# A graph layer and a mixture of experts on one core: stages of a tile closer together, and another list of expert steps

## The chip, the core and the metric

The kernel runs on one core of a Trainium2 chip. The metric is the device time of one execution in microseconds. The core has five engines that run side by side, each in the order of its own instructions: PE (matrix multiply), DVE (vector), ACT (activation), POOL (here it issues the gathers, the read-backs and some stores) and SP (it issues the other transfers).[...]

## What is computed

6250 nodes with 256 features pass a graph layer over 106,250 edges (sorted by target), and then a layer of 8 experts of which each node uses 2:

```python
x = x + gnn(layernorm(x), deg_isqrt, W, b, src, dst)    # h @ W.T + b, gathered by src, summed by dst
x = x + ffn(layernorm(x), Wg, bg, W1, b1, W2, b2)

def ffn(x):
    topk_scores, topk_idx = top_k(x @ Wg.T + bg, 2)
    combine = softmax(topk_scores) spread over the 8 experts
    for e in range(8):
        h = relu(x @ W1[e].T + b1[e])                   # 256 -> 1024
        out = out + combine[:, e] * (h @ W2[e].T + b2[e])
```

All inputs are float32. In the graph layer the sum over edges is taken first and the 256x256 matrix is applied to the sums.

## The kernel before

**Head.** `in_order` counts the degrees, scales the rows and writes them as a table of two float16 halves to DRAM (`ftable`).

**Gathering.** The edges lie in 831 chunks of 128. The loop over the chunk number `s` does for each chunk: `gather` six chunks ahead (POOL, line 404, 128 rows of 1 KB into one of `ROWS` = 24 buffers), `mask` ten chunks ahead (DVE, line 411), and `add_up` (PE, line 418), a matmul of mask and rows that sums the edges of each node in PSUM. Then it issues what was planned for this chunk number, and then pieces of expert work.

**Stages of a tile.** A tile is 128 nodes; there are 49. Tile t is complete at chunk `FROM[t]`, about every 17 chunks. From there its stages are planned at fixed distances in chunks, by `plan_at` and the list `STAGES`:

- `join` (DVE) adds finished windows of the sum, `part_of` (ACT) copies them into a whole tile.
- `turn_sum` (PE) transposes the tile, `keep_turned` (ACT) copies it, `linear` (PE, line 518) applies the matrix and the gate.
- `add_sums`, `guess_root`, `better_root`, `score_nodes`, `choose_experts`, `scale_rows` (all DVE, lines 525 to 582): residual, layer norm, scores, the two experts of each node.
- `rank` (PE, lines 586 and 587): counts per expert, and on ACT a float16 copy of the normalised rows.
- `place_rows`, `place_sorted`, `place_queued`, `mark_slots`, `weigh` (DVE): places in the experts' queues, and a one-hot matrix of sorted slots.
- `sort` (PE, line 650) brings the rows into expert order, `send_rows` copies them (ACT) and writes 64 rows to each expert's queue in DRAM (SP, eight transfers, `fhq`).

`linear` stands 8 chunks before `rank`, `rank` 6 before `sort`, and the rows are sent 24 chunks after `FROM[t]`. The PSUM tile `pt` of `turn_sum`, `linear` and `rank` has one buffer.

**Expert steps.** A step takes up to 128 or 256 rows of one queue. `STREAM` lists the steps of the gathering as (chunk number at which the step is chosen, rows); `TAIL` lists the rows of those chosen after the last tile is sent. `choose` (DVE) takes the expert with most waiting rows. SP then loads the weights (`w1` of 1028 KB by `load_first`, `w2` of 1152 KB by `load_second`, three buffers each) and the rows (`xT` by `load_rows`, after a register load of the column). A step that finds fewer rows than it may take costs the same. The work is cut into pieces: 8 `up` pieces for a step (line 766, with a relu on ACT) and 4 `down` pieces for each 128 rows (line 776); `leave` adds the bias (DVE, line 788) and writes the result to DRAM (`fyq`, SP). `next_kind` alternates the two kinds where both are at hand; where only `down` is, it holds it back when the next `up` is due within `HOLD` = 10 chunks. `earliest` keeps the first `up` of a step at least 13 chunks after its choice and 12 chunks after the last sending that it needs. A credit of `SLOT` = 1250 ns a chunk limits how many pieces are issued.

**Tail.** After chunk 831 the loop goes on with one piece in each round of `s`; planned stages fall due by the same count. `DONE` pairs a step with a tile number: once the step is done, all tiles below the number are taken to be complete. Then `read_back` (POOL, line 859) fetches two expert results for each node, `add_in` (DVE, line 867) adds them, and `store` writes four tiles. `take`, which calls `add_in`, runs in a round where the oldest read-back is eight rounds old, where more than ten are open, or where the `down` pieces of all steps have been issued (`done == USUAL`). Before the last read-backs the kernel checks that no row was written later than `DONE` says; if one was, `any_order`, a slower general program, recomputes everything.

Of the kernel before, what the change touches and what calls it, by code (L numbers as in the profile page):

```python
# [12 lines left out]
SP = mybir.EngineType.SP  # L13
ACT = mybir.EngineType.Activation
AF = mybir.ActivationFunctionType
# [4 lines left out]
P = 128  # L20
N = 6250
NT = 49
# [11 lines left out]
FT = 256  # L34
CAP = 27 * FT
QR = NE * CAP
SLOTS = 64
STREAM = ((74, 128), (83, 128), (94, 128), (103, 128), (112, 128), (121, 128), (130, 128), (139, 128),
          (148, 128), (175, 256), (194, 256), (213, 256), (232, 256), (249, 256), (266, 256), (283, 256),
          (300, 256), (317, 256), (333, 256), (350, 256), (367, 256), (384, 256), (401, 256), (418, 256),  # L40
          (435, 256), (452, 256), (469, 256), (486, 256), (503, 256), (520, 256), (537, 256), (554, 256),
          (572, 256), (589, 256), (606, 256), (623, 256), (640, 256), (657, 256), (674, 256), (691, 256),
          (705, 256), (721, 256), (738, 256), (756, 256), (773, 256), (790, 256), (807, 256), (825, 256),
          (839, 256))
TAIL = (256, 256, 256, 256, 256, 128, 128, 128, 128, 128, 128)
ROWS_OF = [n for s, n in STREAM] + list(TAIL)
USUAL = len(ROWS_OF)
START = [P + sum(ROWS_OF[:step]) for step in range(USUAL + 1)]
# [20 lines left out]
SHARED = 4  # L69
SHIFT = 1.0 / 16  # L70

DONE = ((40, 25), (41, 27), (43, 28), (44, 31), (45, 32), (47, 33), (48, 35), (50, 37), (52, 38), (53, 40),
        (54, 42), (56, 44), (57, 45), (58, 46), (USUAL - 1, NT))
LATER = 1 << 17
TURNED, PLACED, SORTED, SENT = 5, 17, 22, 24
LEAD = (13, 12)
HOLD = 10


COPIES = 3  # L80
# [70 lines left out]
def in_order(ctx: ExitStack, tc: tile.TileContext, g: Shared):  # L151

    nc = tc.nc
# [4 lines left out]
    hq = dram.tile([NE * P, CAP, 2], F32, name="fhq")  # L158
# [209 lines left out]
    t0 = 0  # L368
    for step, t1 in DONE:
        nc.vector.memset(bounds[:, t0:t1, :], float(START[step + 1]))  # L370
# [213 lines left out]
    def rank(r):  # L584
        r.pp = psp.tile([P, 3, NE], F32, name="pt", bufs=1)
        nc.tensor.matmul(r.pp[:, 0], below, r.chose[:, 0], start=True, stop=True)
        nc.tensor.matmul(r.pp[:, 1:3], every, r.chose, start=True, stop=True)
        h2s[r.t] = work.tile([P, 2, D], F16, name="h2s", bufs=3)
        nc.scalar.activation(h2s[r.t][:, 0], r.h2, AF.Copy)

    def place_rows(r):

# [14 lines left out]
    def place_sorted(r):  # L607
        scr = work.tile([P, NE], F32, name="scr")
        r.slotf = work.tile([P, 2], F32, name="slotf")
        for j in range(2):  # L610
            nc.vector.scalar_tensor_tensor(scr, r.sel[:, j], 1.0, r.spot, op0=OP.mult, op1=OP.mult,
                                           accum_out=r.slotf[:, j:j + 1])
        nc.vector.tensor_copy(columns_of[r.t][:, 1], r.totals[0:1, 1])
        if r.t == NT - 1:
            nc.vector.tensor_scalar(r.slotf, r.slotf, dump, None, op0=OP.add)
        nc.scalar.activation(r.ex, r.ex, AF.Exp)

    def place_queued(r):

# [33 lines left out]
    def send_rows(r):  # L653
# [3 lines left out]
        send(r.t)  # L657
        sent += 1

    STAGES = ((9, add_sums), (10, guess_root), (11, better_root, 2), (12, better_root, 1), (12, score_nodes),  # L660
              (13, choose_experts), (14, scale_rows), (16, rank), (PLACED, place_rows), (18, place_sorted),
              (19, place_queued), (20, mark_slots), (21, weigh), (SORTED, sort), (SENT, send_rows))

    def send(t):

# [54 lines left out]
    def load_first(step):  # L720
        f = steps[step]
        f["we"] = nc.values_load(f["go"][0:1, 0:1], engines=(SP,), min_val=0, max_val=(NE - 1) * P)
        f["w1"] = wts.tile([P, W1C], F32, name="w1")
        nc.sync.dma_start(f["w1"], g.W1[bass.ds(f["we"], P), :])

    def load_rows(step):

        f = steps[step]
        assert sent >= f["known"]
        col = nc.values_load(f["go"][0:1, 1:2], engines=(SP,), min_val=0, max_val=CAP - FT)  # L730
        f["xT"] = work.tile([P, FT, 2], F32, name="xT", bufs=4)
        n = ROWS_OF[step]
        nc.sync.dma_start(f["xT"][:, :n, :], hq[bass.ds(f["we"], P), bass.ds(col, n), :])  # L733

    def load_second(step):
        f = steps[step]
        f["w2"] = wts.tile([P, W2C], F32, name="w2")
        nc.sync.dma_start(f["w2"], g.W2[bass.ds(f["we"], P), :])
# [60 lines left out]
    def plan_at(s, fn, *args):  # L799
        tasks.setdefault(s, []).append((fn, args))  # L800

    def run(parts):
        for _ in parts:
            pass

    def in_parts(s, fn, *args):

        def part(s):
            if next(parts, True) is None:
                tasks.setdefault(s + 1, []).insert(0, (part, (s + 1,)))  # L810
        parts = fn(*args)
        plan_at(s, part, s)

    earliest, busy = {}, {}
    taken_up = set()
    for t, s in enumerate(FROM):
        plan_at(s + TURNED, turn_sum, t)
        plan_at(s + TURNED + 1, keep_turned, t)
        plan_at(s + TURNED + 3, linear, t)
        r = Shared()  # L820
        r.t = t
        for at_slot, stage, *args in STAGES:
            plan_at(s + at_slot, stage, r, *args)
        taken_up.update(range(s + SORTED, s + SENT + 1))
        for at_slot, task in ((s + TURNED, "turn_sum"), (s + TURNED + 3, "linear"), (s + PLACED - 1, "rank"),
                              (s + SORTED, "sort")):
            busy[at_slot] = busy.get(at_slot, 0) + TASKS[task]
    for w, (n0, chunks) in enumerate(WINDOWS):
        tasks.setdefault(chunks[-1] + 2, []).insert(0, (join, (w,)))
        plan_at(chunks[-1] + 4, part_of, w)  # L830
    plan_at(3, centre)
    s = 1
    for t in range(0, NT, 2):
# [5 lines left out]
        for at_slot, task in ((s, "inputs_turned"), (s + 2, "inputs_scored")):  # L839
            busy[at_slot] = busy.get(at_slot, 0) + TASKS[task]  # L840
    for step, (s, n) in enumerate(STREAM):
        in_parts(s, fetch, step)
        last = max(t for t in range(NT) if FROM[t] + PLACED < s)
        earliest[step] = max(s + LEAD[0], FROM[last] + SENT + LEAD[1])
    chosen = loaded1 = loaded2 = len(STREAM)
    all_sent = FROM[NT - 1] + SENT + 1

    curu = curd = 0
    done = gone = upped = 0
# [28 lines left out]
    def next_kind(s):  # L878

        first = upped < USUAL and upped <= done + 1 and "xT" in steps.get(upped, {}) and s >= earliest.get(upped, 0)  # L880
        second = done < upped and "w2" in steps.get(done, {})
        if first and second:
            return "down" if was == "up" else "up"
        if first:
            return "up"
        soon = 0 < earliest.get(upped, 0) - s <= HOLD and upped <= done + 1 and curd == 0
        return "down" if second and not soon else None

    def next_piece(s):

# [14 lines left out]
    with tc.manual_schedule():  # L905
# [21 lines left out]
        with tc.tile_pool(name="ftail", bufs=2) as pool:  # L927
            s = NC
            pend = []
            plan = list(DONE)  # L930
            got = asked = allowed = stored = 0
# [12 lines left out]
            while done < USUAL or tasks or len(plan) > 1 or asked < 2 * allowed or pend:  # L944
                for fn, args in tasks.pop(s, []):
                    fn(*args)
                if s > all_sent and s > max(STREAM)[0] + 6:
                    if chosen < min(USUAL, upped + 4):
                        run(choose(chosen))
                        chosen += 1  # L950
                    if loaded2 < min(loaded1, gone + 3):
                        load_second(loaded2)
                        loaded2 += 1
                    if loaded1 < min(chosen, upped + 3):
                        load_first(loaded1)
                        load_rows(loaded1)
                        loaded1 += 1
                over = done
                next_piece(s)
                if done > over:  # L960
                    since[over] = s
                if len(plan) > 1 and done > plan[0][0] and s >= since.get(plan[0][0], 0) + 6 \
                        and asked == 2 * allowed:
                    step, t1 = plan.pop(0)
                    results(allowed, t1, float(START[step + 1]))
                    allowed = t1
                    latest = step
                if asked < 2 * allowed and s % (4 if s > all_sent else 2):
                    pend.append((s, read_back(pool, rowat, asked // 2, asked % 2, latest)))
                    asked += 1  # L970

                if pend and (done == USUAL or len(pend) > 10 or s >= pend[0][0] + 8):
                    take()
                s += 1

# [559 lines left out]
```

## Time and profile before

| | |
|---|---|
| median of 3 timed runs | 1579.9 us (1570.63 to 1580.15) |
| profiled execution, own time | 1342.39 us |
| its span in the trace | 1340.5 us |
| mean granted PE clock in it | 0.959 |
| busy share PE, DVE, ACT, POOL | 86%, 74%, 30%, 67% |
| first and last gather start | 81.7 us, 1126.1 us |
| last segment sum starts on PE | 1136.67 us |

The durations below are those of the profiled execution, which is shorter than the timed runs. "Busy" is the time that an engine spends in instructions; a group of the page is given by line, engine, operation, output and inputs, then its count, its busy time and mean, and the idle time before it with what ended it. Line numbers of the trace are those of the kernel before.

### The profile page before, as it was taken

The page shows a single profiled execution, that of the slowest core. Times are in us where ns is not written, and L with a number is a line of the kernel's source. Part 1 is how long each engine was busy: PE and PEld are TensorE (multiplying, and loading weights), DVE is VectorE, ACT ScalarE, POOL GpSimd, SP SyncE. Part 2 cuts the span into 40 slices and gives each one's busy share as a digit, 9 for nine tenths or more (in the row PEclk, how much of TensorE's full clock was granted, in tenths as well). Part 3 has the DMA queues.
Part 4 walks back from the last instruction along what each step waited for, and adds up shares of the span by engine and source line. Part 5 has one row for each costly group of instructions (what it writes and reads, how often), then busy time and mean ns, then how long its engine had stood idle before and what let it go on. Part 6 is the DMA issues. An engine that isn't in the chain of part 4 may idle for free. (4 is left out here: it accounts for less than half of the span.)

```text
span 1340.5 us, 24208 instructions
## 1 busy us (share of the span) xinstructions
PE 1154.7 (86%) x6304; PEld 896.9 (67%) x6304; DVE 986.4 (74%) x5416; ACT 397.6 (30%) x939; POOL 903.2 (67%) x983
## 2 busy tenths in 40 slices
PE   4439978997879999999989898999999998979992
PEld 4427656774657777676767666767777666868881
DVE  9841668787788888878888887978777775875532
ACT  2622323332323333233323232333222222312230
POOL 2047777777777777777777777777777775557423
PEclk9999867998989999999999999999999998989996
DMA  8343468997778888888888888888888887699783
GB/s 297 112 145 105 121 192 300 337 338 229 226 232 279 262 256 271 252 272 259 256 258 251 268 251 265 257 257 265 255 273 273 252 260 248 218 343 337 272 323 98
DMA packets 159197, 333.81 MB, mean 249 GB/s; under 512 B 26804, under 2 KB 105864, under 8 KB 143688
## 3 DMA queue, kind: packets, MB, share of 16 engines
q1 hardware_dynamic: 111372, 201.66, 44.0%
q0 software_dynamic: 46864, 129.82, 32.8%
q8 instruction: 52, 0.85, 0.3%
q14 instruction: 97, 0.79, 0.2%
q10 hardware_dynamic: 812, 0.68, 0.2%
HBM read 277.55 MB, written 54.50 MB: 248 GB/s over the span
## 5 line engine op out<-in xcount | busy, mean ns | idle before, releaser
L404 POOL DMA_INDIRECT rows<-ftable,src x831 | 790.8, 952 | 253.4 <-issue 115.5
L766 PE MATMUL ph<-xT,w 128*128 128x256 f32 (+1 forms) x1920 | 468.4, 368 | 36.4 <-DMA xT<-fhq 36.1
L776 PE MATMUL py<-w,hid 128*128 128x256 f32 x1680 | 436.9, 383 | 2.3 <-DVE y L788 1.7
L766 PEld LDWEIGHTS ph<-xT,w 128*128 128x128 f32 x1920 | 342.8, 193 | 138.8 <-issue 54.4
L768 ACT ACTIVATE hid<-ph,w 128x256 f32<-128x256 f32 (+1 forms) x480 | 214.3, 447 | 712.9 <-PE ph L766 625.1
L418 PE MATMUL ps<-rows,mask 128*128 128x512 f16 x831 | 309.9, 400 | 79.4 <-DMA rows<-ftable,src 74.6
L776 PEld LDWEIGHTS py<-w,hid 128*128 128x128 f32 x1680 | 317.5, 191 | 86.5 <-issue 20.9
L411 DVE TENSOR_SCALAR mask<-col_b,rel 128x128 f16<-128x128 bf16 x831 | 208.3, 272 | 8.3 <-PE ps L418 8.2
L859 POOL DMA_INDIRECT yb<-fyq,rowat x98 | 94.7, 966 | 84.8 <-issue 33.0
L418 PEld LDWEIGHTS <-mask 128*128 128x128 f16 x831 | 84.6, 105 | 77.4 <-issue 39.9
L788 DVE TENSOR_TENSOR y<-py,w 128x256 f32<-128x256 f32 x105 | 44.3, 422 | 93.9 <-PE py L776 92.3
L867 DVE SCALAR_TENSOR_TENSOR xr<-yb,prob,xr 128x256 f32<-128x256 f32 x98 | 46.0, 482 | 63.2 <-DMA yb<-fyq,rowat 62.5
L485 DVE SCALAR_TENSOR_TENSOR rolled<-rolled,keep,ps 128x256 f32<-128x256 f32 x149 | 70.6, 474 | 14.9 <-PE ps L418 14.8
L500 ACT ACTIVATE whole<-rolled 32x256 f32<-32x256 f32 (+2 forms) x156 | 63.7, 408 | 17.3 <-DVE rolled L488 14.8
L525 DVE SCALAR_TENSOR_TENSOR xr<-pt,norm,xr 128x256 f32<-128x256 f32 x49 | 23.6, 481 | 61.5 <-PE pt L518 61.5
L488 DVE TENSOR_TENSOR rolled<-ps,rolled 128x256 f32<-128x256 f32 x150 | 63.6, 424 | 5.1
L518 PE MATMUL pt<-gw,uT 128*128 128x264 f32 x196 | 54.8, 405 | 0.0
L518 PEld LDWEIGHTS pt<-gw,uT 128*128 128x128 f32 x196 | 39.3, 201 | 16.9 <-issue 6.8
L217 PE MATMUL count<-oh,ol 128*16 128x8 bf16 (+2 forms) x898 | 29.0, 174 | 21.9 <-DVE oh L206 17.9
L461 PEld LDWEIGHTS ph<-wg,turned 128*128 128x128 f32 x196 | 37.2, 279 | 15.4 <-ACT turned L453 14.2
L469 POOL MEMSET keep<- 128x1 f32 x11 | 0.4, 96 | 64.3 <-DMA ftable<-tab 64.3
L217 PEld LDWEIGHTS <-ol 128*16 128x16 bf16 x898 | 28.7, 109 | 22.2 <-DVE ol L203 16.1
(187 smaller groups left out, 1154.7 us busy)
## 6 DMA issues: line engine op xcount, KB each, us to landing
w<-in_W SPq DMA_DIRECT2D x60, 1152.0 KB
w<-in_W SPq DMA_DIRECT2D x60, 1028.0 KB
fhq<-ordered SPq DMA_DIRECT2D x392, 64.0 KB
fyq<-y SPq DMA_DIRECT2D x105, 128.0 KB
rows<-ftable,src POOLq DMA_INDIRECT x831
xT<-fhq SPq DMA_DIRECT2D x45, 256.0 KB
out<-xr POOLq DMA_DIRECT2D x11, 512.0 KB
xr<-in_x SPq DMA_DIRECT2D x6, 896.0 KB
```

The lines of the kernel that those rows point to most:

```text
L217: nc.tensor.matmul(counts[k][:, u - k * GROUP * 8:v - k * GROUP * 8], ol[:, :, i], oh[:, u - first:v - first, i], start=False, stop=(c0 + ...
L404: nc.gpsimd.indirect_dma_start(out=rows[c], out_offset=None, in_=table[:, :], in_offset=bass.IndirectOffsetOnAxis(ap=g.src[:, c:c + 1], ax ...
L411: nc.vector.tensor_scalar(masks[c], g.col_b[:, r:r + P], g.rel[:, c:c + 1], None, op0=OP.is_equal)
L418: nc.tensor.matmul(sums[w], masks.pop(c), rows.pop(c), start=(c == chunks[0]), stop=(c == chunks[-1]))
L485: nc.vector.scalar_tensor_tensor(new, rolled, keeps[kept[w]], ps[:, 0:D], op0=OP.mult, op1=OP.add)
L488: nc.vector.tensor_add(new, ps[:, D:2 * D], new)
L500: nc.scalar.activation(whole[t][p0:p1, :], new[p0:p1, :], AF.Copy)
L518: nc.tensor.matmul(pl, uT[:, k, :], gw[:, k, :], start=(k == 0), stop=(k == 1))
L766: nc.tensor.matmul(ph[:, :n], w1[:, k * H + b * P:k * H + (b + 1) * P], f["xT"][:, :n, k], start=(k == 0), stop=(k == 1))
L768: nc.scalar.activation(f["hid"][:, b, :n], ph[:, :n], AF.Relu, bias=w1[:, 2 * H + b:2 * H + b + 1])
L776: nc.tensor.matmul(f["py"], f["hid"][:, b, a * P:(a + 1) * P], f["w2"][:, b * D:(b + 1) * D], start=(b == 0), stop=(b == HB - 1))
L859: r = nc.gpsimd.indirect_dma_start(out=yb, out_offset=None, in_=yq[0:START[upto + 1], :], in_offset=bass.IndirectOffsetOnAxis(ap=where[:, ...
```

## The change

Each tile's stages follow each other more closely: a tile is sent 17 chunks after `FROM[t]` instead of 24. `linear` stands 2 chunks after `turn_sum` instead of 3, `rank` 6 after `linear` instead of 8, `sort` 4 after `rank` instead of 6. `STREAM` and `TAIL` are replaced: the first step is chosen at chunk 54 instead of 74, eight steps of `STREAM` have 128 rows and 43 have 256 (before 9 and 40), and `TAIL` has six of 256 and three of 128 (before five and six). There are 60 steps as before. `HOLD` is gone. `DONE` has more pairs, and its last one before the end completes tiles 44 to 47 with step 58; one tile is left for after the last step instead of three. `take` waits for `gone`, the steps whose results have been written, instead of `done`. The column of the rows is loaded into its register beside the expert's number, and the exponential of the softmax is issued one stage earlier.

```diff
-STREAM = ((74, 128), (83, 128), (94, 128), (103, 128), (112, 128), (121, 128), (130, 128), (139, 128),
-          (148, 128), (175, 256), (194, 256), (213, 256), (232, 256), (249, 256), (266, 256), (283, 256),
...
-          (839, 256))
-TAIL = (256, 256, 256, 256, 256, 128, 128, 128, 128, 128, 128)
+STREAM = ((54, 128), (60, 128), (72, 128), (91, 128), (100, 128), (109, 256), (124, 256), (139, 256),
+          (155, 256), (171, 256), (187, 256), (209, 256), (226, 256), (243, 256), (260, 256), (277, 256),
...
+          (821, 128), (831, 128), (838, 128))
+TAIL = (256, 256, 256, 256, 256, 256, 128, 128, 128)
...
-DONE = ((40, 25), (41, 27), (43, 28), (44, 31), (45, 32), (47, 33), (48, 35), (50, 37), (52, 38), (53, 40),
-        (54, 42), (56, 44), (57, 45), (58, 46), (USUAL - 1, NT))
+DONE = ((36, 25), (37, 26), (38, 27), (40, 28), (41, 30), (43, 32), (44, 33), (45, 34), (46, 35), (48, 37),
+        (49, 38), (50, 39), (51, 40), (53, 41), (54, 42), (56, 43), (57, 44), (58, 48), (USUAL - 1, NT))
-TURNED, PLACED, SORTED, SENT = 5, 17, 22, 24
+TURNED, PLACED, SORTED, SENT = 4, 13, 16, 17
 LEAD = (13, 12)
-HOLD = 10
...
         nc.scalar.activation(h2s[r.t][:, 0], r.h2, AF.Copy)
+        nc.scalar.activation(r.ex, r.ex, AF.Exp)
...
-        nc.scalar.activation(r.ex, r.ex, AF.Exp)
...
-    STAGES = ((9, add_sums), (10, guess_root), (11, better_root, 2), (12, better_root, 1), (12, score_nodes),
-              (13, choose_experts), (14, scale_rows), (16, rank), (PLACED, place_rows), (18, place_sorted),
-              (19, place_queued), (20, mark_slots), (21, weigh), (SORTED, sort), (SENT, send_rows))
+    STAGES = ((7, add_sums), (8, guess_root), (8, better_root, 2), (9, better_root, 1), (9, score_nodes),
+              (10, choose_experts), (11, scale_rows), (12, rank), (PLACED, place_rows), (14, place_sorted),
+              (14, mark_slots), (15, place_queued), (SORTED, sort), (16, weigh), (SENT, send_rows))
...
+        f["col"] = nc.values_load(f["go"][0:1, 1:2], engines=(SP,), min_val=0, max_val=CAP - FT)
...
-        col = nc.values_load(f["go"][0:1, 1:2], engines=(SP,), min_val=0, max_val=CAP - FT)
...
-        plan_at(s + TURNED + 3, linear, t)
+        plan_at(s + TURNED + 2, linear, t)
...
-        plan_at(chunks[-1] + 4, part_of, w)
+        plan_at(chunks[-1] + 3, part_of, w)
...
-        soon = 0 < earliest.get(upped, 0) - s <= HOLD and upped <= done + 1 and curd == 0
-        return "down" if second and not soon else None
+        return "down" if second else None
...
-                if pend and (done == USUAL or len(pend) > 10 or s >= pend[0][0] + 8):
+                if pend and (gone == USUAL or len(pend) > 10 or s >= pend[0][0] + 8):
```

## The prediction

> **What bounds the kernel now.** I read the page first, then the busy time by stretches, then the timeline of one tile and of the end. From the page:
>
> ```profile
> span 1340.5 us, 24208 instructions
> ...
> PEclk9999867998989999999999999999999998989996
> ...
> L404 POOL DMA_INDIRECT rows<-ftable,src x831 | 790.8, 952 | 253.4 <-issue 115.5
> L766 PE MATMUL ph<-xT,w 128*128 128x256 f32 (+1 forms) x1920 | 468.4, 368 | 36.4 <-DMA xT<-fhq 36.1
> ```
>
> PE has the largest share (86%), but an average over stages hides the pace-maker. A gather takes POOL 0.952 us and the timeline shows 0.30 us before each next one: 1.2525 us a chunk, and 831 chunks make 1041 us. The first gather starts at 81.7 us and the last at 1126.1 us, so POOL never stood for long. The same stretches for all engines, then for L404 alone:
>
> ```profile
> core 0: us, PE busy (x) PEld busy (x) DVE busy (x) ACT busy (x) POOL busy (x), PEclk, DMA share, GB/s
> 185.00:235.00 50.00, 39.54 (x194) 29.88 (x193) 37.67 (x240) 13.51 (x38) 37.98 (x40) 0.76 0.88 285
> 235.00:285.00 50.00, 46.43 (x281) 38.95 (x280) 39.83 (x246) 17.19 (x48) 37.81 (x40) 0.97 0.98 346
> 635.00:835.00 200.00, 183.36 (x859) 138.11 (x858) 167.10 (x938) 61.84 (x147) 151.55 (x160) 1.00 0.82 257
> 1127.00:1187.00 60.00, 51.63 (x231) 41.84 (x230) 47.74 (x288) 15.49 (x38) 25.55 (x28) 0.93 0.74 243
> ```
>
> ```profile
> 85.00:135.00 50.00, 37.81 (x41) 1.00 0.36 103
> 635.00:835.00 200.00, 151.55 (x160) 1.00 0.82 257
> ```
>
> POOL makes 40 or 41 gathers per 50 us everywhere, with DVE at a fifth or at five sixths of its time. So the run has four parts: head (82 us), gathering (to PE's last segment sum at 1136.7 us, POOL's pace), tail (PE, to 1314.4 us) and end (26.1 us).
>
> One tile in the middle, with the stages that the change moves:
>
> ```profile
> 902.30 1.05 PE L518 MATMUL pt<-gw,uT 128*128 128x264 f32 x4
> ...
> 909.92 0.23 DVE L574 SCALAR_TENSOR_TENSOR chose<-col_f,ixf,chose 128x8 bf16<-128x8 f32 x1
> ...
> 912.00 0.17 PE L586 MATMUL pt<-chose,below 128*128 128x8 bf16 x1
> ...
> 912.57 0.15 DVE L598 COPY totals<-pt 128x16 f32<-128x16 f32 x1
> ...
> 915.91 0.48 DVE L638 SCALAR_TENSOR_TENSOR slots<-places,slotf,slots 128x256 f16<-128x256 bf16 x1
> ...
> 918.82 0.60 PE L650 MATMUL px<-slots,h2s 128*128 128x256 f16 x4
> ```
>
> Linear ends at 903.35; DVE has the choice ready 6.8 us later, PE gets to `rank` 8.65 us later. From `rank` to the slots DVE needs 4.4 us, and PE reaches `sort` after 6.8 us. Both waits are covered today, by about 2 us each.
>
> The end, from PE's, DVE's and POOL's timelines:
>
> ```profile
> 1136.67 0.38 PE L418 MATMUL ps<-rows,mask 128*128 128x512 f16 x1
> ...
> 1184.82 2.05 PE L766 MATMUL ph<-xT,w 128*128 128x256 f32 x4 [7.89 <-DMA xT<-fhq]
> ...
> 1310.83 3.61 PE L776 MATMUL py<-w,hid 128*128 128x256 f32 x16
> ```
>
> ```profile
> 1320.26 0.41 DVE L788 TENSOR_TENSOR y<-py,w 128x256 f32<-128x256 f32 x1
> ...
> 1333.08 0.49 DVE L867 SCALAR_TENSOR_TENSOR xr<-yb,prob,xr 128x256 f32<-128x256 f32 x1 [0.65 <-DMA yb<-fyq,rowat]
> ```
>
> PE waits 7.9 us for the first TAIL step's rows, and its last result lies 5.9 us before DVE adds the bias: sums of earlier tiles, which wait for their rows, stand ahead of it.
>
> **The change part by part.** Prices are start to start in the timeline: an `up` piece of 256 rows 0.88 us, of 128 rows 0.46, a `down` piece 0.865, a segment sum 0.205, one tile's own matmuls 1.6.
>
> 1. *Steps moved into the gathering.* I count the pieces of each program before and after the last segment sum. Before: 300 wide ups, 72 narrow, 328 downs, then 60, 48 and 92 in the tail. After: 344, 40 and 357, then 48, 48 and 79. The tail goes from 52.8 + 22.1 + 79.6 = 154.5 us to 42.2 + 22.1 + 68.3 = 132.7 us: **-21.8 us**. The gathering takes 38.7 - 14.7 + 25.1 = 49.1 us more. In all PE does 27 us more, since early steps are taken with fewer rows waiting (13,952 row places instead of 13,440). The 49 us are hidden by POOL's pace: PE's work from the first to the last segment sum, pieces and tile work together, rises from some 870 to 919 us of 1041, which leaves 122 us. If that cover goes, they are paid in full.
>
> 2. *Stages closer.* From linear to `rank` lie 6 chunks instead of 8, from `rank` to `sort` 4 instead of 6. PE runs a chunk in 1.08 us when it does not wait for rows, so 6.5 us stand against DVE's 6.8 and 4.3 against 4.4: it will stand 0 to 0.5 us twice per tile. In the busy stretch from 200 to 310 us, some six tiles, DVE needed 6.0 to 9.0 us and 5.5 to 8.8 us, so there it stands 1 to 7 us per tile. Over 49 tiles: 7 us at least, 85 us at most; I take the middle, 45. That is less than the 122 us of cover: **0**. Behind a waiting `rank` or `sort` stand the next segment sums; only when PE is 24 chunks (`ROWS`), 30 us, behind the gathers does POOL wait for a buffer. The largest lag now is 12.9 us.
>
> 3. *The early stretch.* From chunk 60 to 200 PE would need 159 us at full clock (34 more than now), against 175 us of gathers. The granted clock was 0.76 at 185 to 235 us. [...] I take 0, and keep +10.
>    The transfers there get lighter: a narrow step every 9 chunks loads 2.2 MB per 11.3 us, 198 GB/s beside 105 for the gathers, which is how 346 GB/s came about; a wide one every 15.5 chunks loads 115 GB/s.
>
> [...]
>
> 5. *The last tile's chain in the tail.* There a chunk's place is taken by one piece. From linear to `rank` of tile 48 lie 3.6 us of pieces instead of 7, and from `rank` to `sort` 2.7 instead of 5.2, while DVE needs 6.8 and 4.4 plus some sums of 0.4 us. PE stands about 4.5 and 2.5 us there, and some at tile 47, against about 1 now: **+7 us** (0 to +11). PE reaches `sort` of tile 48 two to three us sooner, and the rows of the first TAIL step land at about 1182 instead of 1184.8 us: the wait of 7.9 us stays.
>
> 6. *Fewer narrow TAIL steps* (3, were 6). The last six took 53 us for 6 x 7.14 = 43 us of PE work, as 2.2 MB per step compete with the read-backs. Half of them go: **-2 us** (0 to -5).
>
> 7. *The end.* With `gone` in place of `done` the last bias add no longer stands behind sums (-5.5 us). Tiles 44 to 47 are then read behind step 58: 8 read-backs at 1.25 us from about 2 us before PE's end, the last summed 10 us after it; then tile 48's two, to 15 us, and the store as now 7 us: 22 instead of 26.1 us, **-4 us** (0 to -6).
>
> 8. *The rest.* The second register load beside the first, `Exp` beside the copy on ACT (30% busy), no holding back of second layers: 0; SP has no wait in the chain but for data, and ACT's cover is a piece of PE.
>
> Sum: -21.8 + 7 - 2 - 4 = -20.8. A second way, along the last tile: rows 2.7 us sooner, then 108.7 instead of 119.5 us of pieces, -2, -4: -19.5. I take -20: the profiled execution's 1342.4 us becomes 1322.4, -1.5%. The median of the timed runs is 1579.9 us, 1.177 times the profiled one. The page does not say why; engine-bound stages would all stretch alike, so I carry the ratio: **1556 us**.
>
> **The rivals.** A measurement of this kernel can tell about 1% from no change.
> - *PE becomes the pace-maker (slower).* At `rank` and `sort` PE stands so long that it falls 30 us behind the gathers. It decides once the stand is over 122 / 49 = 2.5 us per tile. For it: tiles at 200 to 310 us need up to 9 us. Against: the later tiles are steady at 6.6 and 4.4. At 3.5 us per tile, 171 - 122 = 49 us are added: 1342.4 - 20 + 49 = 1371 us, 1614 us timed.
> - *Hidden anyway (within 1%).* The last tile's chain sets when the TAIL may begin. If its rows land no sooner and the end keeps its 26 us, the gain is 10.8 us, 1567 us; the same if POOL loses 10 us in the early stretch. For it: the standing wait of 7.9 us.
> - *More than forecast.* No stands at the last tiles, TAIL rows 6 us sooner, narrow steps -5, end -6: -39 us, 1534 us.
> - *It does not hold its own bounds.* A row written after the step that `DONE` names would start the fallback, whose 831 gathers and 831 scatters at 0.95 us are 1.6 ms more. Counted from the given inputs, tiles 44 to 47 need step 58 and get 58; no bound is passed. Under 1%.
>
> **How the numbers follow.** Forecast with its better end 53%, hidden 27%, PE as pace-maker 20%. The range goes from the better end, 1534, to a PE that stands 3.3 us per tile: 162 - 122 = 40 us, 1362 us, 1604 us timed.
>
> **What would show it.** Right: POOL still at 40 gathers per 50 us and the last gather at about 1126 us; PE waits at L585 and L649 of 20 to 60 us; tail of about 160 us instead of 177.7; the last bias add within 1 us of PE's last matmul. Wrong: gathers that wait for PE's segment sums, a last gather after 1135 us, or a first TAIL step that waits over 15 us for its rows.

## The result, and the profile after

The change made the kernel **slower**: 1624.99 us (median of 4, 1619.61 to 1632.5) against 1577.69 us (median of 4, 1570.63 to 1580.15), ratio 1.0316 [1.0278, 1.0354]. The forecast was 1556 us with a range of 1534 to 1604. The rival "PE becomes the pace-maker" came true.

One fact must come first. The runs fell on several chips, and there are two kinds. On two of them the kernel before takes 1338 to 1340 us, on three others 1575 to 1598 us, and in the comparison above 1578. By their times, the trace that the prediction read (1342 us) came from the first kind and the runs that it was scaled to from the second. Below, every ratio compares runs of one chip; "the 1338 us chips" and "the 1575 us chips" name the kinds. On a 1338 us chip the change is worse: e8_after 1431.74 against 1340.06 us, ratio 1.0693 [1.0665, 1.0721].

The page of the kernel after, profiled at 1625.04 us, on a 1575 us chip (the lines of after named below are those of before minus 1; the last three columns of a group are its busy time, the mean, and its idle time with what ended it):

```profile
span 1623.2 us, 24366 instructions
...
PEclk9999689999979888989898989889899999988997
...
L403 POOL DMA_INDIRECT rows<-ftable,src x831 | 791.4, 952 | 509.1 <-PE ps L417 271.9
L765 PE MATMUL ph<-xT,w 128*128 128x256 f32 (+1 forms) x1920 | 535.6, 414 | 50.9 <-issue 22.9
...
L585 PE MATMUL pt<-chose,below 128*128 128x8 bf16 x49 | 8.8, 180 | 133.8 <-DVE chose L571 66.9
```

The same page of the same kernel on a 1338 us chip (e8_after), the like of the trace shown of before:

```profile
span 1427.3 us, 24366 instructions
...
PEclk9999699999898999999998999999999999989997
...
L403 POOL DMA_INDIRECT rows<-ftable,src x831 | 790.8, 952 | 342.8 <-issue 149.0
L765 PE MATMUL ph<-xT,w 128*128 128x256 f32 (+1 forms) x1920 | 513.4, 401 | 17.8 <-DMA xT<-fhq 16.6
...
L585 PE MATMUL pt<-chose,below 128*128 128x8 bf16 x49 | 8.6, 176 | 83.7 <-DVE chose L571 83.5
```

A gather still takes 0.952 us, but POOL's idle time ahead of it rose from 253 to 343 us here and to 509 us there. Most of the rise is waiting for PE's segment sums: 56 us of it in e8_before, 136 in e8_after, 272 in the first page. And `rank` (L585), which had no row on the page of before, waits 84 or 134 us for the choice of experts. The stretches of e8_after:

```profile
core 0: us, PE busy (x) PEld busy (x) DVE busy (x) ACT busy (x) POOL busy (x), PEclk, DMA share, GB/s
185.00:235.00 50.00, 43.80 (x277) 36.03 (x276) 38.79 (x236) 17.80 (x50) 37.89 (x40) 0.98 0.94 301
235.00:285.00 50.00, 48.95 (x249) 38.32 (x248) 37.27 (x226) 16.56 (x41) 38.03 (x40) 1.00 0.89 275
635.00:835.00 200.00, 176.93 (x766) 133.12 (x765) 142.31 (x811) 56.87 (x133) 132.05 (x140) 0.92 0.72 223
```

From 635 to 835 us POOL makes 140 gathers, not 160; PE is busy 177 us, but at 0.92 of its clock and with 766 matmuls instead of 859. One tile of that stretch on PE:

```profile
792.86 1.05 PE L517 MATMUL pt<-gw,uT 128*128 128x264 f32 x4
...
796.77 1.03 PE L417 MATMUL ps<-rows,mask 128*128 128x512 f16 x4
800.43 0.18 PE L585 MATMUL pt<-chose,below 128*128 128x8 bf16 x1 [2.63 <-DVE chose L571]
800.83 0.17 PE L586 MATMUL pt<-chose,every 128*128 128x16 bf16 x1 [0.22 <-DVE chose L573]
800.93 4.55 PE L765 MATMUL ph<-xT,w 128*128 128x256 f32 x12
...
805.53 1.06 PE L765 MATMUL ph<-xT,w 128*128 128x256 f32 x4
```

This is the whole story of a tile. Linear ends at 793.9. DVE has the choice ready 6.5 us later, where 6.8 were forecast. But PE has no expert work for the last chunks: **four segment sums stand back to back** at 796.77 with no piece between them, and PE stops for 2.63 us. Then its matmuls run slower: 12 up records take 4.55 us, where 4 take 1.06 a moment later.

### The profile page after: what moved, and what is told of

Read it like the earlier page. It is cut to its first block, busy times and chain, and to the rows that moved or that the text cites. A ratio compares the mean times of both kernels' runs of the same rounds, so it can differ in the third digit from the quotient of the medians.

```text
span 1623.2 us, 24366 instructions
## 1 busy us (share of the span) xinstructions
PE 1259.2 (78%) x6368; PEld 959.1 (59%) x6368; DVE 987.3 (61%) x5428; ACT 400.3 (25%) x939; POOL 903.6 (56%) x983
## 4 chain that ended last, share of the span: by engine, by line
PE 62%; DVE 19%; issue 8%; another core or an unknown queue 4%; DMA 2%; ACT 2%; SPq 1%; POOL 1%; ACTq 0%; POOLq 0%; DVEq 0%
PE ph L765 25%; PE py L775 18%; PE ps L417 9%; PE pt L517 3%; PE ph L460 2%; DVE rs L546 2%; DVE mask L410 2%; PE px L649 1%; DVE ry L547 1%; DVE xr L524 1%; SPq L672 1%; DVE rolled L487 1%; DVE y L787 1%; PE px L449 1%
## 5 line engine op out<-in xcount | busy, mean ns | idle before, releaser
L765 PE MATMUL ph<-xT,w 128*128 128x256 f32 (+1 forms) x1920 | 535.6, 414 | 50.9 <-issue 22.9
L765 PEld LDWEIGHTS ph<-xT,w 128*128 128x128 f32 x1920 | 386.4, 216 | 170.1 <-issue 60.8
L775 PE MATMUL py<-w,hid 128*128 128x256 f32 x1744 | 454.0, 386 | 0.0
L775 PEld LDWEIGHTS py<-w,hid 128*128 128x128 f32 x1744 | 330.6, 193 | 71.5 <-issue 2.4
L410 DVE TENSOR_SCALAR mask<-col_b,rel 128x128 f16<-128x128 bf16 x831 | 198.0, 269 | 32.9 <-remote 17.9
L585 PE MATMUL pt<-chose,below 128*128 128x8 bf16 x49 | 8.8, 180 | 133.8 <-DVE chose L571 66.9
L585 PEld LDWEIGHTS <-below 128*128 128x128 bf16 x49 | 5.0, 103 | 134.7 <-DVE chose L571 68.7
L460 PE MATMUL ph<-wg,turned 128*128 128x8 f32 x196 | 38.5, 324 | 36.8 <-ACT turned L452 24.2
```

The lines of the kernel that those rows point to most:

```text
L410: nc.vector.tensor_scalar(masks[c], g.col_b[:, r:r + P], g.rel[:, c:c + 1], None, op0=OP.is_equal)
L460: nc.tensor.matmul(px[:, t - t0], xT[:, k, (t - t0) * P:(t - t0 + 1) * P], wg[:, k, :], start=(k == 0), stop=(k == 1))
L765: nc.tensor.matmul(ph[:, :n], w1[:, k * H + b * P:k * H + (b + 1) * P], f["xT"][:, :n, k], start=(k == 0), stop=(k == 1))
L775: nc.tensor.matmul(f["py"], f["hid"][:, b, a * P:(a + 1) * P], f["w2"][:, b * D:(b + 1) * D], start=(b == 0), stop=(b == HB - 1))
```

## The experiments

The theories named in the expectations: A, the closer stages make PE stand at `rank` and `sort`, and PE sets the pace. Its rivals: the lists of steps, or slower gathers, or an early standstill (in the first trace of after PE, ACT and DVE stand between 100 and 127 us). Later A was split: D, the distance itself costs; E, what costs is that the chunks ahead of `rank` carry no piece.

**Which part of the change.** The kernel before again, for its trace (e1_before); after with the stage distances of before (e2_wide); before with the stage distances of after (e3_close):

```diff
-TURNED, PLACED, SORTED, SENT = 4, 13, 16, 17      # e2_wide; e3_close is the reverse, on before
+TURNED, PLACED, SORTED, SENT = 5, 17, 22, 24
-        plan_at(s + TURNED + 2, linear, t)
+        plan_at(s + TURNED + 3, linear, t)
...
```

> The kernel before once more, to get a trace of it at its timed 1578 us; the only trace so far took 1342. Theory A (two regimes: PE, once it is 24 chunks behind the gathers, waits for DVE at rank and sort in every tile and does not catch up): such a trace shows a lag of 30 to 40 us, gathers at 1.50 to 1.55 us per chunk waiting for PE's segment sums, a last gather at 1330 to 1360 us, and waits of PE at L586 and L650 in the lagged stretch of at most 60 us, against 134 at L585 in the kernel after. Theory B (the timed runs only have slower gathers or a slower chip): lag under 15 us, POOL busy all the time, its gathers at 1.15 us or longer each. If the profiled run falls at 1342 again, the two stay open.

> The kernel after with the stage distances of before alone put back (TURNED, PLACED, SORTED, SENT = 5, 17, 22, 24, the list STAGES, linear 3 behind turn_sum, part_of 4 behind its window); lists of steps, DONE, gone and the rest as after. Theory A: the closer stages are what costs, so 1545 to 1580 us, waits at L585 down from 134 to under 60 us. Rival (the lists of steps cost: 27 us more PE work that is no longer hidden, more work early): 1605 to 1630 us, waits at L585 stay over 100.

> The kernel before with the stage distances of after alone (TURNED, PLACED, SORTED, SENT = 4, 13, 16, 17, the list STAGES, linear 2 behind turn_sum, part_of 3 behind its window); lists of steps, HOLD, DONE as before. Theory A: 1600 to 1640 us, PE waits at L586 of 110 to 150 us. Rival (lists): 1570 to 1590 us.

All ran on a 1338 us chip. e1_before: 1338.28 us, ratio 0.9998 [0.9987, 1.0008], so it left the question of the 1578 us open. e2_wide: 1328.69 us, 0.9933 [0.9913, 0.9954]. e3_close: 1425.94 us, 1.0662 [1.0628, 1.0696]. On this kind of chip the stages alone make the loss; all the rest of the change is a small gain. Neither e2_wide nor e3_close was run on a 1575 us chip. The waits of PE in e3_close (tile and line, what it waited for: us in all, times, the longest):

```profile
PE px L650 <- DVE slots L638: 48.3, 27, 2.8
PE pt L586 <- DVE chose L572: 46.0, 31, 5.8
...
PE px L650 <- DVE h2s L633: 25.2, 34, 1.2
```

Here the greater part of the stand is at `sort`, and no early standstill was needed: PE fell back tile by tile, from 9 us behind the gathers at chunk 24 to 35 us at chunk 280.

**Which of the seven chunks.** After (e4_after), after with `rank` 8 behind `linear` (e5_rank8), with `sort` 6 behind `rank` (e6_sort6), and with 7 and 5 (e7_mid):

```diff
-TURNED, PLACED, SORTED, SENT = 4, 13, 16, 17
+TURNED, PLACED, SORTED, SENT = 4, 15, 18, 19      # e5_rank8
+TURNED, PLACED, SORTED, SENT = 4, 13, 18, 19      # e6_sort6
+TURNED, PLACED, SORTED, SENT = 4, 14, 18, 19      # e7_mid
...
```

> The kernel after once more, to see it where the kernel before takes 1338 us. Theory A (the stands at rank and sort exceed the cover of POOL's pace and PE sets the pace; no early standstill is needed for it, as the run of the closer stages alone showed): 1338 + 88 for the stages - 9 for the rest = 1417 us, a lag that grows tile by tile to 30 us, and 100 to 140 us of waits at L585 and L649. Rival (the standstill of all engines at 100 to 127 us in the first trace of after put it behind, and without it POOL keeps the pace): 1322 to 1345 us.

> The kernel after with rank 8 chunks behind linear again instead of 6, and what follows rank moved with it (PLACED 15, SORTED 18, SENT 19); sort stays 4 behind rank. Theory A with sort as the dearer place (74 of 129 us of stand in the run of the closer stages alone): some 70 us of stand at sort, of which about 40 are covered, 1350 to 1370 us. Theory A with rank as the dearer place: 1322 to 1340 us.

> The kernel after with sort 6 chunks behind rank again instead of 4 (SORTED 18, SENT 19); rank stays 6 behind linear. Theory A with sort as the dearer place: 55 us of stand at rank, nearly all covered, 1325 to 1345 us. With rank as the dearer place: 1360 to 1400 us.

> The kernel after with one chunk more at each place: rank 7 behind linear, sort 5 behind rank (PLACED 14, SORTED 18, SENT 19). Theory A as a threshold (the chunks between must hold as much PE time as DVE's chain, 6.8 and 4.4 us at 1.08 us a chunk, so 7 and 5 are enough): 1322 to 1340 us and under 30 us of stand. Rival (every chunk taken away costs its part): half of what after loses, 1365 to 1385 us.

These ran on a 1575 us chip (before 1574.63 us): after 1.0336 [1.0296, 1.0377], rank8 1.0206 [1.0134, 1.0278], sort6 1.0036 [1.001, 1.0061], mid 1.0468 [1.042, 1.0517]. The expected times were for the other chips; what can be held against them is the order. sort6, which still stands 84 us at `rank`, is the fastest, and mid, with a chunk more at each place, the slowest. But mid is no test of the distance. It stands little at `rank` (10.5 us), and 155 us at first up pieces whose rows have not landed, and this comes of its own edit: most steps are chosen 14 chunks after `FROM[t]`, and with `PLACED` = 14 such a step takes rows of tile t, while `earliest`, which counts only tiles with `FROM[t]` + `PLACED` below the choice, leaves that tile out. Its first up then stands 8 chunks behind the sending of its rows instead of 12 (in the trace at chunk 10 of the next tile, in sort6 at 14).

**Three chunks kept, four given back.** e8_free3 leaves `rank` 8 behind `linear` and `sort` 6 behind `rank`, but keeps the other three chunks of the change; before, after and wide ran beside it.

```diff
-TURNED, PLACED, SORTED, SENT = 4, 13, 16, 17
+TURNED, PLACED, SORTED, SENT = 4, 15, 20, 21
...
```

> The kernel before once more for its trace. The kernel before has taken 1338 us in one set of runs and 1575 us in others. In the traces of the variants of after from the 1575 us set, DVE stood 67 to 134 times for over 0.3 us on nothing but its own previous result (44 to 119 us in all); in the 1338 us set never. If this run falls in the 1575 us set: theory A expects the same stops of DVE in before (40 or more), a PE lag of 25 us or more and gathers that wait for PE's segment sums; the rival (slower gathers or matmuls) a lag under 15 us. If it takes 1338 us: no such stop.

> The kernel after beside before, the wide and the free version on the same chip. Where before takes 1338 us: theory A 1417 us (1338 + 88 for the stages - 9 for the rest), a lag growing tile by tile; rival (only the 1575 us set makes PE the pace-maker): 1322 to 1345 us. Where before takes 1575 us: 1625 us again.

> The kernel after with the stage distances of before. Where before takes 1338 us: 1329 us again. Where it takes 1575 us: theory A (the distances carry the loss in both sets) 1555 to 1580 us; rival (there the lists of steps cost, since PE's 27 us more work are no longer hidden) 1590 to 1610 us.

> The kernel after with rank 8 behind linear and sort 6 behind rank as in before, but the other three of the seven chunks taken away as in after (turn_sum 4 behind FROM, linear 2 behind turn_sum, sent 1 behind sort: PLACED 15, SORTED 20, SENT 21). Theory A (only the four chunks between linear, rank and sort cost): within 0.5% of the wide version, 1320 to 1335 us where before takes 1338. Rival (any chunk taken from the chain of a tile costs): 30 to 40 us above the wide version.

All on a 1338 us chip: before 1340.06 us (e8_before, one run, 1340.42), after 1.0693 [1.0665, 1.0721], wide 0.9942 [0.992, 0.9963], free3 1322.93 us, **0.9873 [0.9853, 0.9892]**, and again 0.9863 [0.9832, 0.9893] in e11_free3. So giving back the four chunks between `linear`, `rank` and `sort` takes the whole loss away, and the other three are a gain of 0.7%. The edit also moves pieces: with `PLACED` = 15 a step chosen 14 chunks after `FROM[t]` no longer takes tile t's rows, and its first up goes from chunk 12 of the next tile (after) to 10 (free3, and wide and rank8 too). What is distance and what is the order of the pieces is not parted by it. The waits of after, and those of free3:

```profile
PE pt L585 <- DVE chose L571: 83.5, 37, 4.9
PE ps L417 <- DMA rows<-ftable,src: 31.5, 4, 28.8
```

```profile
PE ps L417 <- DMA rows<-ftable,src: 62.9, 44, 28.8
PE ph L765 <- DMA xT<-fhq: 18.6, 6, 8.1
...
PE pt L585 <- DVE chose L571: 7.2, 5, 3.2
```

In free3 PE waits for rows 44 times, all but the first, of 28.8 us, short: it keeps up with POOL, which is what a kernel at POOL's pace looks like. In after only the 28.8 us before the first row and three more are left.

**Where the empty chunks lie.** The program itself shows why PE has nothing to do just ahead of `rank`. A tile has some 17 chunks and a step 16 pieces; some chunks carry two pieces, and three to five per tile none. Most of the empty ones lie just ahead of the first `up` of the next step, which `earliest` allows at `FROM` + `SENT` + 12. With `SENT` = 24 that is chunk 2 of the tile after next, with 17 it is chunk 12 of the next tile: the chunk of `rank`. In after the empty chunks are 9, 10 and 11. Counted over tiles 12 to 43, PE has 7.9 pieces between `linear` and `rank` in before, 8.1 in wide and 3.6 in after; in e3_close, with the other lists, the empty chunks lie at 13, 14 and 15, ahead of `sort`, which is where it stood. e9_lead19 and e9_lead16 move them and nothing else:

```diff
-LEAD = (13, 12)
+LEAD = (13, 19)      # e9_lead19: empty chunks at 16, 0, 1;  e9_lead16, 16: at 13, 14, 15
```

> The kernel after with LEAD = (13, 19) instead of (13, 12) and nothing else: every stage stays as close as in after, but the first up of a step may start 7 chunks later, so the chunks without a piece lie at 16, 0 and 1 instead of 9, 10 and 11. Theory E (the empty chunks ahead of rank cost): PE work between linear and rank 6.1 pieces x 0.87 + 6 x 0.21 = 6.5 us against DVE's 6.5, waits at L585 under 25 us, 1325 to 1350 us where before takes 1338 (1560 to 1595 us where it takes 1575). Theory D (the distance itself): waits at L585 of 80 us or more, 1420 to 1440 us (1620 to 1635).

> The kernel after with LEAD = (13, 16): the empty chunks lie at 13, 14 and 15, just ahead of sort. Theory E: the stand moves from rank to sort, L585 under 25 us, L649 100 to 180 us (1.7 pieces x 0.87 + 4 x 0.21 = 2.3 us against 4.2 to 6 us of DVE), 1390 to 1460 us where before takes 1338. Theory D: as after, L585 80 us or more and L649 under 20 us.

> The kernel before for its trace, should it fall in the slower set (about 1575 us): then 40 or more stops of DVE of over 0.3 us on its own previous result, a PE lag of 25 us or more and gathers waiting for PE's segment sums. At 1338 us: none of it, as in e1_before.

These ran on a 1575 us chip (before 1598.2 us): lead19 1.0235 [1.0141, 1.033], lead16 1.0366 [1.0281, 1.0451]. The stand moved as E says: at `rank` 142 us in e4_after, 41 and 58 here; at `sort` 14, 85 and 135. But the time hardly followed. e10_before took 1590.45 us and is read in the next section. lead19 then ran on a 1338 us chip, and free3 once more:

> The kernel after with LEAD = (13, 19) once more. Where before takes 1338 us: theory E (empty chunks ahead of rank) waits at rank under 25 us, those at sort up to 30 us (4.0 pieces x 0.87 + 4 x 0.21 = 4.3 us of PE work against 4.2 to 6 us of DVE), 1330 to 1365 us; theory D (distance itself) 1420 to 1440 us with 80 us or more at rank. In the slower set 1.01 to 1.03 times before again.

> The version with three chunks taken away once more (rank 8 behind linear, sort 6 behind rank). Where before takes 1338 us: 1323 us again. In the slower set: 0.98 to 1.00 times before if only the four chunks cost there too; over 1.01 if late hand-overs make each chunk of distance count.

e11_lead19: 1409.01 us, 1.0545 [1.0507, 1.0582]. **Both E (up to 1365) and D (from 1420) missed.** Its waits, and two stands of one tile:

```profile
PE ph L765 <- ACT hid L767: 50.4, 25, 2.5
PE px L649 <- DVE h2s L632: 47.0, 35, 2.2
...
PE pt L585 <- DVE chose L571: 21.9, 13, 3.5
```

```profile
703.68 0.50 PE L649 MATMUL px<-slots,h2s 128*128 128x256 f16 x3 [1.60 <-DVE h2s L632]
704.02 0.81 PE L417 MATMUL ps<-rows,mask 128*128 128x512 f16 x3
704.67 1.97 PE L765 MATMUL ph<-xT,w 128*128 128x256 f32 x8
708.83 1.17 PE L765 MATMUL ph<-xT,w 128*128 128x256 f32 x4 [2.19 <-ACT hid L767]
```

The stand at `rank` fell from 93 to 27 us with the distance unchanged, so the place of the empty chunks does decide which hand-over stands (E). But the place tried here is not harmless either (D): PE now stands 55 us at `sort`, and the first up pieces 53 us, 50 of them for a relu on ACT. In the tile above that relu is queued behind `part_of`, which waits for DVE's `join`:

```profile
707.86 0.41 ACT L499 ACTIVATE whole<-rolled 32x256 f32<-32x256 f32 x1 [2.96 <-DVE rolled L487]
```

A stand of PE is thus replaced by another hand-over, two engines away.

**The last two,** one for each kind of chip:

> The kernel after with rank 8 chunks behind linear, sort 4 behind rank, for the 1338 us set. PE then has 6.3 pieces between linear and rank, 6.3 x 0.87 + 8 x 0.21 = 7.1 us against DVE's 6.5, and 5.0 pieces between rank and sort, 5.0 x 0.87 + 4 x 0.21 = 5.2 us against 4.2 to 6 us. If the rank hand-over carries the loss: rank under 15 us, sort 20 to 50 us, within the cover of some 60 us, 1320 to 1345 us. If sort 4 behind rank costs by itself: 1365 to 1400 us.

> The version with three chunks taken away, for the slower set: 0.98 to 1.00 times before if only the four chunks cost there too, over 1.01 if late hand-overs make each chunk of distance count. In the 1338 us set 1320 us a third time.

Both ran on a 1575 us chip (before 1578.14 us): rank8 1.0113 [1.0085, 1.0141], free3 1.0102 [1.0049, 1.0154]. So free3, the best version on the 1338 us chips, is about 1% slower than before on these, where after is about 3% slower. By these ratios, which are of different chips, giving back the four chunks takes some two thirds of the loss away there (giving back two, in sort6, more), and what makes the rest is not shown. How rank8 and sort6 do on a 1338 us chip was not measured.

PE's stands by place and its busy time, in us, summed from the waits of each trace:

| kernel (kind of chip) | rank | sort | ups | rows | busy | span |
|---|---|---|---|---|---|---|
| e8_before (1338) | 8 | 5 | 54 | 60 | 1154 | 1339 |
| e8_wide | 6 | 3 | 30 | 67 | 1166 | 1328 |
| e8_free3 | 9 | 4 | 25 | 65 | 1166 | 1321 |
| e8_after | 93 | 11 | 18 | 35 | 1217 | 1427 |
| e3_close | 56 | 74 | 9 | 38 | 1184 | 1421 |
| e11_lead19 | 27 | 55 | 53 | 31 | 1186 | 1408 |
| e10_before (1575) | 28 | 10 | 116 | 55 | 1229 | 1589 |
| e4_after | 142 | 14 | 63 | 49 | 1259 | 1624 |
| e5_rank8 | 5 | 50 | 154 | 41 | 1249 | 1587 |
| e6_sort6 | 84 | 6 | 111 | 32 | 1248 | 1580 |
| e12_free3 | 11 | 20 | 173 | 32 | 1270 | 1600 |

From wide to after on one chip the span grows by 99 us: 87 at `rank`, 7 at `sort`, 51 in longer matmuls, less 32 and 13 that PE had waited for rows and for `xT`: 100.

## Why the prediction was wrong

- **Step 1, steps moved into the gathering: the tail was right, the cover was mis-sized.** From the last segment sum to PE's end, before took 177.8 us (e8_before); after takes 159.9 (forecast "about 160 us"), as these lines of e8_after show, of PE and then of DVE:

```profile
1245.54 0.38 PE L417 MATMUL ps<-rows,mask 128*128 128x512 f16 x1
1253.53 0.19 PE L585 MATMUL pt<-chose,below 128*128 128x8 bf16 x1 [3.71 <-DVE chose L571]
...
1291.35 1.14 PE L765 MATMUL ph<-xT,w 128*128 128x256 f32 x4 [3.55 <-DMA xT<-fhq]
...
1401.78 3.61 PE L775 MATMUL py<-w,hid 128*128 128x256 f32 x16
```

```profile
1405.43 0.42 DVE L787 TENSOR_TENSOR y<-py,w 128x256 f32<-128x256 f32 x1 [4.59 <-PE py L775]
```

  But "which leaves 122 us" counted PE's work at start-to-start prices and full clock. The row beside it said 183.36 us busy of 200: over 1041 us that leaves 87, and 38 once the 49 us are in. Used up were 45 (32 + 13 above).
- **Step 2, stages closer: the step that failed, with the cover of step 1 and the clock of step 3.** DVE's 6.8 us were right (6.5 to 6.9 in the steady tiles). "PE runs a chunk in 1.08 us" holds for a chunk with a piece in it; an empty one takes 0.21. The mean of six chunks was used where three of the six are empty in after, which the order of the program shows without a run. 3.6 x 0.87 + 6 x 0.21 = 4.4 us of PE work against 6.5 gives 2.1 us per tile; measured were 93 us at `rank` over 49 tiles, 1.9 each. I took 45 for both places from a range of 7 to 85.
- **Step 3, the early stretch: the 0 was right on a 1338 us chip, and the clock was missing where it counted.** In e8_after the granted clock there was 0.98 and 1.00, and POOL made 40 gathers in each 50 us, as in before. The 10 us kept beside the 0 were the author's estimate, and no run shows them: in the trace of the first page the clock there was 0.69 and 0.96 and POOL made 33 and 31 gathers, but a standstill of PE, ACT and DVE lies ahead of it. And the step priced no clock for the stands of step 2: 51 us (PE busy 1217 us in e8_after, 1166 in e8_wide, at a granted clock of 0.92 and 1.00 from 635 to 835 us).
- **The gathers beside a busier DVE: no longer.** In the trace of before a gather took 945 ns on the mean from 100 to 134 us, with DVE busy 6.5 us of 34, and 950 ns from 800 to 1000 us, with DVE busy 162 us of 200. Over all 831 the mean was 952 ns there, in the trace of the first page and in e8_after, and 951 in e10_before.
- **Step 5, the last tiles: right for the stands, wrong for the rows.** PE stands 3.71 + 0.28 + 2.77 + 0.47 = 7.2 us at the last two ranks; before 0.5. But the wait for the first TAIL rows fell to 3.6 us, where 7.9 were expected.
- **Step 6, narrow steps** was not measured apart. Of the 10 us between its 53 and 43, the trace of before shows 2.1 us of PE's waits for transfers (1.56 for rows, 0.56 for weights) and 1.7 for DVE; that the read-backs make the rest is not shown.
- **Step 7, the end: right.** The last bias add starts with PE's end, at 1405.4 us, and the end takes 21.9 us (22 forecast; 26.1 before).
- **The scaling.** "Engine-bound stages would all stretch alike" is wrong. Against e8_before, the trace of before on such a chip (e10_before) still has gathers of 951 ns, and DVE and ACT are busy no longer (980 and 392 us, in e8_before 986 and 398). PE is busy 75 us more, at a granted clock of 0.912 instead of 0.954, and idle 175 us more:

```profile
L404 POOL DMA_INDIRECT rows<-ftable,src x831 | 789.9, 951 | 459.0 <-issue 185.1
L766 PE MATMUL ph<-xT,w 128*128 128x256 f32 (+1 forms) x1920 | 498.5, 385 | 116.4 <-issue 49.6
```

  PE is 34 us behind the gathers at chunk 10 (9.5 in e8_before) and 24 to 39 us from chunk 24 on, at the limit of `ROWS`, in the kernel before already. It falls back in a standstill that each of the ten traces from 1575 us chips has and none from the others. ACT copies what PE had ready at 99.4 us only at 109.9, and stands again:

```profile
109.93 0.60 ACT L453 ACTIVATE turned<-px 128x512 f32<-128x512 f32 x1 [14.59 <-remote]
127.38 0.18 ACT L463 ACTIVATE xg<-ph 128x16 f32<-128x16 f32 x1 [16.85 <-remote]
```

  So in this trace POOL does not set the pace, and the cover that the forecast leaned on is not there. The prediction says what follows: "If that cover goes, they are paid in full", 49 us. Whether they make the 1% of free3 there was not tested. The standstill is not needed for the loss, since e8_after has none.
- The forecast's 1322.4 us for a chip like the traced one is what free3 reaches (1322.9), with a tail of 160.0 us and an end of 21.9: the gain was there, and the four chunks between `linear`, `rank` and `sort` took 109 us (e8_after less e8_free3). That the two totals agree so closely is in part luck, since free3 has no 7 us of stands at the last tiles.

## What to carry to other kernels

Before stages that hand work between two engines are moved closer, count what the waiting engine has to do between them in the order of its own program: an average per chunk hides the chunks that are empty, and the distances can move the empty ones (here through `earliest`) to the very place where the wait is. Price a stand on PE twice, once for the stand and once for the slower matmuls that may follow it (in e8_after 12 up records in 4.55 us behind a stand of 2.63 us). And ask that the trace comes from a run whose time is the timed one; where it does not, the regime may differ, not the scale.

## What the runs showed of the hardware

**The clock after a stand.** In e8_after all 16 stands of 2.63 to 2.75 us at `rank` in the gathering, and all five of 2.09 and 2.10 us, were followed by up matmuls at 0.43 us start to start instead of 0.22. In e11_lead19, 12 stands of 1.58 to 1.62 us at `sort` cost no clock, and of 13 of 2.18 and 2.19 us at up pieces only two did, so the length of a stand alone does not decide. In that kernel two short stands cost less clock than one long one in after: its clock was 1.00 from 635 to 835 us with PE busy 170 us of 200, that of after 0.92 with 177. The granted clock itself, in the trace of the first page: behind a stand of 3.29 us that ends at 617.1 us it is 0.53 from 617.6 to 621.0 us, in which time fall most of 12 up records of 4.45 us, and 1.00 from 621.0 to 622.0 us. In e8_after a stand of 2.09 us, with 0.2 to 0.4 us more between the two small matmuls of `rank`, was followed by the slower matmuls each time.

**On some chips an engine starts late although what it waits for is done.** I counted the DVE instructions that wait for nothing but DVE's own earlier result (some 4,500 per run after 85 us) and started over 0.3 us after it. On the 1338 us chips there is none in nearly every trace, never more than one. On the 1575 us chips there are 67 in e4_after (55 us in all), 153 in e12_free3 (115 us) and 169 in e10_before (141 us), the longest 2.75 us. One of them in e10_before:

```profile
454.55 0.22 DVE L573 TENSOR_SCALAR chose<-col_f,ixf 128x8 bf16<-128x8 f32 x1
456.61 0.23 DVE L574 SCALAR_TENSOR_TENSOR chose<-col_f,ixf,chose 128x8 bf16<-128x8 f32 x1 [1.83 <-remote]
```

Nothing stands between the two instructions, and in e8_before and e8_after the gap at this place is 0.04 us. None of these stops lies in the first 190 us of the three runs, so the standstill before 128 us is a case of its own. What causes either, and why on some chips only, was not found; that they are why before takes 1575 us there is argued from the traces, not shown by an experiment.
